# Seven 128-cubed zone products for each 256-cubed block product in two of three weight slices

## The chip, the cores and the metric

The kernel runs on one core of one Trainium2 chip. The metric is device time in microseconds, the median of several executions. One more execution is taken with the hardware profiler, and all views come from it.

## What is computed

One layer over 128 graphs of 128 nodes and 768 features, 12 heads of 64, all in fp32. The kernel's heads and weights are those of this reference, cut to what matters:

```python
h = jnp.maximum(_layernorm(x, axis=-1), 0.0)
q, k, v = (split_heads(h @ W + b) for W, b in ((Wq, bq), (Wk, bk), (Wv, bv)))   # W: 768 x 768
scores = einsum('bhqd,bhkd->bhqk', q, k) / 8 + beta * adj
scores = where(adj > 0, scores, -9e15)
out = einsum('bhqk,bhkd->bhqd', softmax(scores), v)
x = x + merge_heads(out)
```

## The kernel before

Four graphs make a group, and `direct` loops over 32 groups `G`. A group's activations are 512 rows of 768, cut into 2 x 3 blocks of 256 (`A00` to `A12`, held transposed). The weights are used in three slices of 768 columns: `qk0` (the first three 128-column blocks of Wq and of Wk side by side), `v`, and `qk1` (the other half of Wq and Wk). Each slice is cut into 3 x 3 blocks of 256 (`B00` to `B22`).

A slice takes 15 block products in place of 18 (`PRODUCTS`): sums of activation blocks (`SUMS_A`, made on VectorE by `sum_acts`, one set a group) are multiplied by sums of weight blocks (`SUMS_B`, made once, by `sum_weights` on VectorE or, for part of `qk0`, by accumulating DMAs on GpSimd's queue in `sum_by_dma`, and kept in SBUF). A product is added to one or two of the six results, with a sign. Products of one of four chains `a` to `d` add up in one PSUM bank, and after each product the partial sum of its chain goes out (`product`, L404 the matmuls): the first of a result by ScalarE with the bias (L426; for V by VectorE, L416), the others by VectorE adds into SBUF (L432, L421). Group 0 does its first slice as 18 plain products (`plain_slice`, L612) while the sums are being made.

The order within a slice is written by hand: after the product at position n, the functions listed in `todo[n]` are called. So the score matmuls of the slice before (`scores`, L454) come at position 1 of the next slice, followed by VectorE's cap and bias (L458) and ScalarE's exponentials (L461); the products of probabilities with V (`attend`, L494) are interleaved with matmuls of the slice by `turn()`, then come the division (L475, ScalarE's L478 in group 0), the residual add on GpSimd (L503) and the store (L504). The next group's rows are loaded (`load_x`, L162), normalised by ScalarE in place (`norm`, L334), transposed by VectorE (`to_hT`, L341) and summed (L347). From group 3 on the row statistics come from separate loads (`load_halves`, L301), and `row_moments` (called at the last position of `qk0`) spreads mean and scale over the partitions by 16 small DMAs (`block<-row`, L325).

A scheduler turns this into one queue for each engine: among the instructions that are ready it takes the one that comes first in the code, unless `tc.issue_after` puts it behind another; waits and buffer slots follow from the tiles. DMAs are issued from SyncE's queue (SP) but for a few; a DMA waits in that queue for the slot that it writes and for what it reads.

Of the kernel before, what the change touches and what calls it, by code (L numbers as in the profile page):

```python
# [17 lines left out]
P = 128  # L18
HEADS = 12
GRP = 4  # L20
# [11 lines left out]
def kernel(  # L32
# [64 lines left out]
BY_DMA = (  # L97
    ("T10", (None, "B12")), ("T2", ("B01", "B02", "B22")), ("T6", ("B00", "B02", "B22")), ("T0", (None, "B00")),
    ("T11", ("B11", "B12")),
)  # L100
DONE_BY_DMA = (1, 2, 3, 4, 6, 11)


# [7 lines left out]
AV_AT = (5, 8, 11)  # L111
WARM = 13

# [4 lines left out]
SUMS_AT = (5, 9, 6, 6, 7, 8, 9, 10, 11, 13, 14)  # L118


@with_exitstack
def direct(ctx, tc, x, adj, wq, bq, wk, bk, wv, bv, beta, out, bad):
# [27 lines left out]
    stat = ctx.enter_context(tc.tile_pool(name="stat", bufs=4))  # L150
    psum = ctx.enter_context(tc.tile_pool(name="psum", bufs=1, space=bass.MemoryType.PSUM))
# [4 lines left out]
    xg, A, biasT, vt, qk = {}, {}, {}, {}, {}  # L156

    def load_x(G, g, engines):
        t = xg[G, g] = work.tile([P, NB, QD], F32, tag="x", name=f"x_{G}_{g}")
        src = x[G * GRP + g].rearrange("(b i) (a f) -> a i b f", i=SQ, a=NB)  # L160
        for a in range(NB):
            engines[a % len(engines)].dma_start(t[a * SQ:(a + 1) * SQ], src[a])  # L162


    for g in range(2):
        t = xg[0, g] = work.tile([P, NB, QD], F32, tag="x", name=f"x_0_{g}")
# [16 lines left out]
    vring = [const.tile([P, 2 * GRP, VE], F32, name=f"v{i}") for i in range(7)]  # L183
# [5 lines left out]
    def load_block(sl, k, j, t, add=False):  # L189
        def part(w, at, n):  # L190
            return w.rearrange("(p c) n -> p c n", c=NC)[:, 2 * k:2 * k + 2, at:at + n]

        if sl == "v":
            nc.sync.dma_start(t, part(wv, j * 2 * P, 2 * P))
        else:
            oc = j + 3 * int(sl[2])
            for i, w in enumerate((wq, wk)):
                if add:
                    nc.gpsimd.dma_start(t[:, :, i * P:(i + 1) * P], part(w, oc * P, P), accum_op=ALU.add)
                else:  # L200
                    nc.sync.dma_start(t[:, :, i * P:(i + 1) * P], part(w, oc * P, P))

    def load_weights(sl, blocks=[f"B{k}{j}" for j in range(3) for k in range(3)]):
        for b in blocks:
            t = const.tile([P, 2, H2], F32, name=f"{sl}_{HOME.get(b, b)}")
            load_block(sl, int(b[1]), int(b[2]), t)
            wt[sl, b] = t

    def sum_by_dma(sl, step):

        for name, blocks in BY_DMA:
            if step < len(blocks):
                if (sl, name) not in wt:
                    raw = [r for r, home in HOME.items() if home == name]
                    wt[sl, name] = wt[sl, raw[0]] if raw else const.tile([P, 2, H2], F32, name=f"{sl}_{name}")
                b = blocks[step]
                if b:
                    load_block(sl, int(b[1]), int(b[2]), wt[sl, name], step > 0)

    def sum_weights(sl, n):  # L220
        name, a, b, sign = SUMS_B[n]
        if sl == "qk0" and n in DONE_BY_DMA:
            return
# [3 lines left out]
        if a[0] == "-":  # L227
            nc.vector.scalar_tensor_tensor(wt[sl, name], wt[sl, a[1:]], -1.0, wt[sl, b], op0=ALU.mult,
                                           op1=ALU.add if sign > 0 else ALU.subtract)
        else:  # L230
            nc.vector.tensor_tensor(wt[sl, name], wt[sl, a], wt[sl, b], ALU.add if sign > 0 else ALU.subtract)
# [11 lines left out]
    bqk = const.tile([P, 2, NC], F32, name="bqk")  # L243
# [92 lines left out]
    def to_hT(G, r, k):  # L336
        name = f"A{r}{k}"
        t = A[G, name] = work.tile([P, 2, H2], F32, tag=name, name=f"{name}_{G}", bufs=1 + (name in ("A01", "A02")))
        for g in range(2):
            src = xg[G, 2 * r + g].rearrange("p b (j c) -> p c b j", c=NC)[:, 2 * k:2 * k + 2]  # L340
            last = nc.vector.transpose(t[:, :, g * N:(g + 1) * N].rearrange("p c (b i) -> p c b i", i=SQ), src)  # L341
        return last

    def sum_acts(G, n):
# [3 lines left out]
        A[G, name] = t  # L348

# [37 lines left out]

    def product(G, sl, n, order):
# [8 lines left out]
        for i in range(2):  # L397
            for c in range(2):
                if sl == "v":
                    lhs, rhs = a[:, c, i * N:(i + 1) * N], b[:, c, :]  # L400
                else:
                    lhs, rhs = b[:, c, i * P:(i + 1) * P], a[:, c, :]
# [4 lines left out]
        for (r, j), sign in uses:  # L407
            key = (G, sl, r, j)
            if sl == "v":
                got = p.rearrange("p g (h d) -> p (g h) d", d=HD)  # L410
                if key not in vt:
                    vt[key] = vring[nv[0] % len(vring)]
                    nv[0] += 1
                    o4 = vt[key].rearrange("p (g h) e -> p g h e", g=2)[:, :, :, 0:HD]
                    bias = bv_b[:, j * 2 * P:(j + 1) * 2 * P].rearrange("p (h d) -> p h d", d=HD)
                    added[G] = nc.vector.tensor_tensor(o4, bias[:, None, :, :].to_broadcast([P, 2, 4, HD]),  # L416
                                                        p.rearrange("p g (h d) -> p g h d", d=HD),
                                                        ALU.add if sign > 0 else ALU.subtract)
                else:
                    o = vt[key][:, :, 0:HD]  # L420
                    added[G] = nc.vector.tensor_tensor(o, o, got, ALU.add if sign > 0 else ALU.subtract)  # L421
            elif key not in qk:
                t = qk[key] = work.tile([P, 2, H2], F32, tag="qk", name=f"{sl}_{G}_{r}_{j}", bufs=8)
# [19 lines left out]
    def scores(G, u):  # L443

        order = (3 * u, 3 * u + 2, 3 * u + 1)
        ps = {(oc, i): take() for oc in order for i in range(2)}
        for oc in order:
            for g in range(GRP):
                t = qk[G, f"qk{u}", g // 2, oc % 3]
                at = slice((g % 2) * N, (g % 2 + 1) * N)  # L450
                for i in range(2):
                    r = slice(i * HD, (i + 1) * HD)
                    for k in range(0, N, HD):
                        nc.tensor.matmul(ps[oc, i][k:k + HD, g * N:(g + 1) * N], t[r, 1, at][:, k:k + HD], t[r, 0, at],  # L454
# [10 lines left out]
    def weigh(G, oc, r, pa, o):  # L465
# [7 lines left out]
        def divide():  # L473
            if G:
                nc.vector.tensor_mul(o, pa[:, :, 0:HD], t[:, 1, :, None].to_broadcast([P, 4, HD]))  # L475
            else:
                for b in range(4):
                    nc.scalar.activation(o[:, b], pa[:, b, 0:HD], AF.Copy, scale=t[:, 1, b:b + 1])  # L478
# [106 lines left out]
    def attention(G, u):  # L585

        todo = {}
        for i, oc in enumerate((3 * u, 3 * u + 2, 3 * u + 1)):
            todo.setdefault(AV_AT[i] - 3, []).append(lambda oc=oc: load_xo(G, oc))
            todo.setdefault(AV_AT[i], []).append(lambda oc=oc: attend(G, oc))  # L590
        return todo

# [6 lines left out]
    def plain_slice(G, sl, todo):  # L599

        n = 0
        for r in range(2):
            for j in range(3):
# [3 lines left out]
                parts = (slice(0, N), slice(N, H2)) if r == j == 0 else (slice(0, H2),)  # L607
                for at, k in [(at, k) for at in parts for k in range(3)]:
                    a, b = A[G, f"A{r}{k}"], wt[sl, f"B{k}{j}"]
                    for i in range(2):  # L610
                        for c in range(2):
                            last = nc.tensor.matmul(p[:, i, at], b[:, c, i * P:(i + 1) * P], a[:, c, at],  # L612
                                                    start=(k == 0 and i == 0 and c == 0), stop=(c == 1),
                                                    skip_group_check=True)
# [5 lines left out]
                    if k == 2:  # L620
                        t = qk[G, sl, r, j] = work.tile([P, 2, H2], F32, tag="qk", name=f"{sl}_{G}_{r}_{j}", bufs=8)
                        oc = j + 3 * int(sl[2])
                        for i in range(2):
                            nc.scalar.activation(t[:, i, :], p[:, i, :], AF.Identity, bias=bqk[:, i, oc:oc + 1])
# [33 lines left out]
    def rows_2(g, mv, r):  # L658

        v = xg[0, g].rearrange("p b (j c) -> p c (b j)", c=NC)  # L660
        for k in range(3):
            n = work.tile([P, 2, P], F32, tag="e", name=f"rows_{g}_{k}", bufs=6)
            first["dve"] = nc.vector.tensor_scalar(n, v[:, 2 * k:2 * k + 2], mv[:, 0:1], r, op0=ALU.subtract,
# [22 lines left out]
    def second():  # L686
# [5 lines left out]
        nc.scalar.copy(bqk.rearrange("p i c -> p (i c)"), bank[:, 0:2 * NC])  # L692
        give(bank)

# [48 lines left out]
    for G in range(NG):  # L743
        todo = attention(G - 1, 1) if G else {}
# [9 lines left out]
        if G:  # L754
            todo.setdefault(SC_AT, []).insert(0, lambda: scores(G - 1, 1))
# [13 lines left out]
        if not G:  # L769
# [4 lines left out]
            for n in range(len(SUMS_A)):  # L774
                then(n + 5, lambda n=n: after(sum_acts, 0, n))
            for n in range(len(SUMS_B)):
                then(n // 2 + 5, lambda n=n: after(sum_weights, "v", n))
            plain_slice(0, "qk0", todo)
        else:
            if G == 1:  # L780
                for n in range(8, len(SUMS_B)):
                    then(n - 7, lambda n=n: behind_scores(sum_weights, "qk0", n))
                then(4, lambda: behind_scores(bias_2, 1, early[1]))
            slice_of(G, "qk0", todo)
        todo = {SC_AT: [lambda: scores(G, 0)]} if G else {}
        if G + 1 < NG:
# [13 lines left out]
            else:  # L800
                for n in range(len(SUMS_B)):
                    then(n, lambda n=n: behind_adds(sum_weights, "qk1", n))
                then(8, lambda: sum_by_dma("qk0", 0))
                then(10, lambda: early.append(behind_adds(bias_1, 0, adj_0)))
        slice_of(G, "v", todo)
# [180 lines left out]
```

## Time and profile before

| | |
|---|---|
| time, median of 3 runs | 2881.66 us (2881.62 to 2881.95) |
| profiled execution: span from first to last instruction | 2879.8 us |
| time of the profiled execution itself | not given beside its span; the median lies 1.9 us above the span |
| TensorE, weight loads, VectorE, ScalarE, GpSimd busy | 100%, 70%, 69%, 28%, 12% |
| DMA | 220.93 MB, 77 GB/s in the mean |

In the views below, a line of the groups or the timeline names the source line (L404 is line 404 of the kernel), the engine (PE TensorE, PEld its weight loads, DVE VectorE, ACT ScalarE, POOL GpSimd, SPq SyncE's DMA queue), the operation, and result <- inputs with shapes. In the groups there follow count, busy us, mean ns of one, and the engine's idle time just before with what ended most of it. In the timeline the first two numbers are the start and the length in us of a run of like instructions. In the busy times by stretch the columns are stretch, its length, then busy us and count of PE, PEld, DVE, ACT, POOL, then granted clock, DMA share and GB/s.

### The profile page before, as it was taken

The page shows a single profiled execution, that of the slowest core. Times are in us where ns is not written, and L with a number is a line of the kernel's source. Part 1 is how long each engine was busy: PE and PEld are TensorE (multiplying, and loading weights), DVE is VectorE, ACT ScalarE, POOL GpSimd, SP SyncE. Part 2 cuts the span into 40 slices and gives each one's busy share as a digit, 9 for nine tenths or more (in the row PEclk, how much of TensorE's full clock was granted, in tenths as well). Part 3 has the DMA queues.
Part 4 walks back from the last instruction along what each step waited for, and adds up shares of the span by engine and source line. Part 5 has one row for each costly group of instructions (what it writes and reads, how often), then busy time and mean ns, then how long its engine had stood idle before and what let it go on. Part 6 is the DMA issues. An engine that isn't in the chain of part 4 may idle for free.

```text
span 2879.8 us, 81472 instructions
## 1 busy us (share of the span) xinstructions
PE 2871.1 (100%) x35321; PEld 2010.1 (70%) x35321; DVE 1972.8 (69%) x4511; ACT 815.4 (28%) x1755; POOL 333.4 (12%) x319
## 2 busy tenths in 40 slices
PE   9999999999999999999999999999999999999999
PEld 7766667666676666767667766677666676666766
DVE  7867667676666666666766667667676676766665
ACT  1522222232332323313232232322222222323321
POOL 3111011110111110110101101011010111101100
PEclk9999999999999999999999999999999999999999
DMA  8222223222232222332223322233222232222311
GB/s 203 77 61 78 64 79 84 79 69 69 74 87 82 65 71 69 88 86 64 75 70 82 86 65 79 64 82 84 69 79 61 81 84 78 69 68 74 86 39 43
DMA packets 417363, 220.93 MB, mean 77 GB/s; under 512 B 109148, under 2 KB 416616, under 8 KB 417000
## 3 DMA queue, kind: packets, MB, share of 16 engines
q1 hardware_dynamic: 412864, 213.45, 27.4%
q8 instruction: 277, 4.54, 0.7%
q0 software_dynamic: 3808, 1.84, 0.5%
q14 instruction: 86, 0.70, 0.1%
q10 hardware_dynamic: 328, 0.40, 0.1%
HBM read 164.76 MB, written 50.33 MB: 75 GB/s over the span
## 4 chain that ended last, share of the span: by engine, by line


## 5 line engine op out<-in xcount | busy, mean ns | idle before, releaser
L404 PE MATMUL bank<-S,qk_T 128*64 128x256 f32 x7056 | 867.5, 380 | 0.0
L432 DVE TENSOR_TENSOR qk<-qk,bank 128x512 f32<-128x512 f32 (+1 forms) x631 | 425.2, 674 | 395.9 <-PE bank L404 394.0
L426 ACT ACTIVATE qk<-bank,bqk 128x256 f32<-128x256 f32 x756 | 316.5, 470 | 1132.7 <-PE bank L404 946.8
L494 PEld LDWEIGHTS bank<-v,e 128*64 128x64 f32 x6048 | 433.2, 137 | 220.4
L404 PEld LDWEIGHTS bank<-S,qk_T 128*64 128x64 f32 x7056 | 454.7, 137 | 173.3 <-ACT e L461 5.2
L404 PE MATMUL bank<-S,qk_B 128*64 128x256 f32 x4032 | 543.5, 380 | 0.3 <-ACT qk L426 0.3
L503 POOL TENSOR_TENSOR xo<-xo,o 128x512 f32<-128x512 f32 x189 | 252.6, 1336 | 2258.0 <-DVE o L475 1587.6
L404 PE MATMUL bank<-A,qk_T 128*64 128x256 f32 x4032 | 490.1, 379 | 0.0
L494 PE MATMUL bank<-v,e 128*64 128x65 f32 x6048 | 430.8, 221 | 0.0
L404 PE MATMUL bank<-v_T,S 128*64 128x256 f32 x3584 | 421.4, 380 | 0.0
L461 ACT ACTIVATE e<-e 128x512 f32<-128x512 f32 x378 | 227.8, 629 | 655.1 <-DVE e L458 654.5
L421 DVE TENSOR_TENSOR v<-v,bank 128x512 f32<-128x512 f32 x320 | 219.9, 687 | 233.0 <-PE bank L404 231.2
L404 PEld LDWEIGHTS bank<-v_T,S 128*64 128x64 f32 x3584 | 254.6, 137 | 130.4 <-issue 5.7
L404 PEld LDWEIGHTS bank<-A,qk_T 128*64 128x64 f32 x4032 | 262.8, 137 | 100.8 <-issue 0.2
L458 DVE SCALAR_TENSOR_TENSOR e<-bank,biasT 128x512 f32<-128x512 f32 x378 | 231.7, 681 | 85.2 <-PE bank L454 85.2
L404 PEld LDWEIGHTS bank<-S,qk_B 128*64 128x64 f32 x4032 | 236.2, 138 | 56.2 <-ACT qk L426 0.7
L404 PE MATMUL bank<-v_B,S 128*64 128x256 f32 x2048 | 243.2, 379 | 0.0
L404 PE MATMUL bank<-v_T,A 128*64 128x256 f32 x2048 | 238.1, 379 | 0.0
L334 ACT ACTIVATE x<-x,block 128x192 f32<-128x192 f32 x464 | 217.7, 536 | 63.3 <-DMA block<-row 60.3
L341 DVE STREAM_TRANSPOSE A<-x 128x256 f32<-128x256 f32 x378 | 213.1, 610 | 4.0 <-ACT x L334 3.9
L404 PEld LDWEIGHTS bank<-v_T,A 128*64 128x64 f32 x2048 | 147.3, 137 | 73.7
L404 PEld LDWEIGHTS bank<-v_B,S 128*64 128x64 f32 x2048 | 147.2, 137 | 73.6
(102 smaller groups left out, 1665.5 us busy)
## 6 DMA issues: line engine op xcount, KB each, us to landing
x<-in_x_dram SPq DMA_DIRECT2D x504, 96.0 KB, 2.6
xo<-in_x_dram SPq DMA_DIRECT2D x189, 256.0 KB, 3.0
out_dram<-xo SPq DMA_DIRECT2D x189, 256.0 KB, 2.4
half<-in_x_dram SPq DMA_DIRECT2D x232, 192.0 KB, 2.4
adj<-in_adj_dram SPq DMA_DIRECT2D x128, 64.0 KB, 2.4
block<-row SPq DMA_DIRECT2D x464, 1.0 KB, 1.7
qk_T<-in_L_gnn_Wq_dram SPq DMA_DIRECT2D x13, 128.0 KB, 4.1
qk_T<-in_L_gnn_Wk_dram SPq DMA_DIRECT2D x13, 128.0 KB, 4.5
```

The lines of the kernel that those rows point to most:

```text
L334: nc.scalar.activation(t, t, AF.Relu, bias=shift[G, n], scale=rstd[G, n])
L341: last = nc.vector.transpose(t[:, :, g * N:(g + 1) * N].rearrange("p c (b i) -> p c b i", i=SQ), src)
L404: nc.tensor.matmul(p[q:q + HD, i, :], lhs[:, q:q + HD], rhs, start=(first and i == 0 and c == 0), stop=(c == 1), skip_group_check=True)
L421: added[G] = nc.vector.tensor_tensor(o, o, got, ALU.add if sign > 0 else ALU.subtract)
L426: opened[0] = nc.scalar.activation(t[:, i, :], p[:, i, :], AF.Identity, bias=bqk[:, i, oc:oc + 1], scale=float(sign))
L432: added[G] = nc.vector.tensor_tensor(t[:, :, cols], t[:, :, cols], p[:, :, cols], ALU.add if sign > 0 else ALU.subtract)
L458: taken[0] = nc.vector.scalar_tensor_tensor(e, ps[oc, i].rearrange("p (g n) -> p g n", g=GRP), SCORE_CAP * ISCALE, biasT[G], op0=ALU.min, ...
L461: nc.scalar.activation(e, e, AF.Exp, scale=1.0 / ISCALE)
L494: nc.tensor.matmul(pa[q:q + HD, 2 * g + i, :], es[G, oc, i][:, 2 * r + g, q:q + HD], vt[G, "v", r, h // 4][:, 4 * g + h % 4, :], start=Tru ...
L503: nc.gpsimd.tensor_add(t, t, o.rearrange("p a (b j) d -> p (a b) (j d)", j=2))
```

## The change

In groups 1 to 31 the slices `qk0` and `v` are done by `slice_z` and `product_z`: a 256-cubed product is cut once more into 2 x 2 x 2 blocks of 128 and done as seven 128-cubed products ("zones") in place of eight. Four sums of 128 x 128 activation blocks are made per product on GpSimd (`inner`, called in the `qk1` slice before), the seven weight zones of a product (`T`, 128 x 7 x 128) are prepared in group 0 (`prepare`: VectorE's sums, ScalarE's copies, four GpSimd sums each), stored to a DRAM buffer (`kept`) and streamed back for each product (`load_T`) through five slots. A chain has two PSUM banks; the zones are summed apart over the whole slice, and `decode` on GpSimd combines the seven zones of a finished result into its four blocks. Group 0's `v` slice becomes plain. The features are assigned to partitions in another order, so each weight part is loaded by four DMAs of 32 rows and a pair of graphs is transposed in one instruction. The sums by DMA go, the division is done by ScalarE in all groups, and scores and attention come in another order and somewhat later. The diff, cut to its core:

```diff
-BY_DMA = (...)
+AV_Z = (7, 9, 12)
+ZORDER = (0, 4, 2, 8, 1, 6, 5, 3, 10, 7, 13, 9, 11, 12, 14)
+RING = 5
+INNER_AT = ((5, (1, 11, 12)), (6, (0,)), (7, (4, 2)), (8, (5,)), (9, (6,)), (10, (8, 3, 9)), (11, (7,)), (12, (10,)),
+            (14, (13, 14)))
...
+    def load_part(w, k, at, n, t):
+        src = w.rearrange("(a c j) n -> a j c n", a=NB, j=SQ)
+        for a in range(NB):
+            nc.sync.dma_start(t[a * SQ:(a + 1) * SQ], src[a][:, 2 * k:2 * k + 2, at:at + n])
...
+        def home(n):
+            return work.tile([P, 7, P], F32, tag="T", name=f"prep_{sl}_{n}", bufs=RING)
+        def rest(n, t):
+            e = nc.gpsimd
+            e.tensor_tensor(t[:, 2], t[:, 4], t[:, 1], ALU.subtract)
+            e.tensor_tensor(t[:, 6], t[:, 1], t[:, 0], ALU.subtract)
+            e.tensor_tensor(t[:, 1], t[:, 4], t[:, 6], ALU.subtract)
+            e.tensor_tensor(t[:, 5], t[:, 3], t[:, 1], ALU.subtract)
+            k = kept[sl, n] = dram.tile([P, 7, P], F32, name=f"kept_{sl}_{n}")
+            nc.sync.dma_start(k, t)
...
+    ring = [(G, sl, n) for G in range(1, NG) for sl in ("qk0", "v") for n in ZORDER]
+    def load_T():
+        if nt[0] < len(ring):
+            G, sl, n = ring[nt[0]]
+            nt[0] += 1
+            t = tz[G, sl, n] = work.tile([P, 7, P], F32, tag="T", name=f"T_{G}_{sl}_{n}", bufs=RING)
+            nc.sync.dma_start(t, kept[sl, n])
...
+    def inner(G, n):
+        a = A[G, PRODUCTS[n][0]]
+        t = SP[G, n] = work.tile([P, GRP, P], F32, tag=f"SP{ZORDER.index(n)}", name=f"SP{n}_{G}", bufs=1)
+        e = nc.gpsimd
+        e.tensor_tensor(t[:, 0], a[:, 0, N:H2], a[:, 1, N:H2], ALU.add)
+        e.tensor_tensor(t[:, 1], t[:, 0], a[:, 0, 0:N], ALU.subtract)
+        e.tensor_tensor(t[:, 2], a[:, 0, 0:N], a[:, 0, N:H2], ALU.subtract)
+        e.tensor_tensor(t[:, 3], a[:, 1, 0:N], t[:, 1], ALU.subtract)
...
+    def product_z(G, sl, n):
...
+        acts = (a[:, 0, 0:N], s[:, 1], s[:, 2], a[:, 1, 0:N], s[:, 3], a[:, 1, N:H2], s[:, 0])
+        for z in range(7):
+            lhs, rhs = (acts[z], b[:, z]) if sl == "v" else (b[:, z], acts[z])
+            for q in range(0, P, HD):
+                nc.tensor.matmul(p[z // 4][q:q + HD, z % 4, :], lhs[:, q:q + HD], rhs, start=(first and z % 4 == 0),
+                                 stop=True, skip_group_check=True)
+            turn()
+        load_T()
...
+                t = qk[key]
+                nc.vector.tensor_tensor(t[:, 0:4], t[:, 0:4], p[0], op)
+                added[G] = nc.vector.tensor_tensor(t[:, 4:7], t[:, 4:7], p[1][:, 0:3], op)
+            left[key] -= 1
+            if not left[key]:
+                decode(G, sl, r, j)
...
+    def decode(G, sl, r, j):
+        def twice(z):
+            return t[:, z:z + 1].to_broadcast([P, 2, P])
+        if sl != "v":
+            e.tensor_tensor(t[:, 1:4:2], t[:, 1:4:2], twice(0), ALU.add)
+            e.tensor_tensor(t[:, 2:5:2], t[:, 2:5:2], twice(1), ALU.add)
+            e.tensor_tensor(t[:, 4], t[:, 4], t[:, 6], ALU.add)
+            e.tensor_tensor(t[:, 5:7], t[:, 5:7], twice(2), ALU.add)
+            return
...
-            if G:
-                nc.vector.tensor_mul(o, pa[:, :, 0:HD], t[:, 1, :, None].to_broadcast([P, 4, HD]))
-            else:
-                for b in range(4):
-                    nc.scalar.activation(o[:, b], pa[:, b, 0:HD], AF.Copy, scale=t[:, 1, b:b + 1])
+            for b in range(4):
+                nc.scalar.activation(o[:, b], pa[:, b, 0:HD], AF.Copy, scale=t[:, 1, b:b + 1])
...
         if G:
-            todo.setdefault(SC_AT, []).insert(0, lambda: scores(G - 1, 1))
+            for n, order in ((1, (2, 0)), (2, (1,))):
+                todo.setdefault(n, []).insert(0, lambda order=order: scores(G - 1, 1, order))
...
-            slice_of(G, "qk0", todo)
+            slice_z(G, "qk0", todo)
...
+            for at, ns in INNER_AT:
+                for n in ns:
+                    then(at, lambda n=n: inner(G + 1, n))
```

More of the change, by code (lines that the diff above doesn't have):

```diff
@@ L408, in product @@
             key = (G, sl, r, j)
[L409 to L423, printed above, removed]
+            if key not in qk:
+                t = qk[key] = home_qk(*key)
                 oc = j + 3 * int(sl[2])
@@ L773, in direct, with step @@
             then(4, lambda: half(2))
[L774 to L777, printed above, removed]
+            prep = deque(prepare("qk0") + prepare("v"))
+            def step(behind, count):
+                for _ in range(count):
+                    if prep:
+                        behind(prep.popleft())
+            for n in range(5, 18):
+                then(n, lambda n=n: step(after, 1 + n % 2))
             plain_slice(0, "qk0", todo)
```

254 lines of the change are left out of this document (178 added, 76 removed).

## The prediction

> **What bounds the kernel now.** First the page: the span and the busy shares, then the groups.
>
> ```profile
> PE 2871.1 (100%) x35321; PEld 2010.1 (70%) x35321; DVE 1972.8 (69%) x4511; ACT 815.4 (28%) x1755; POOL 333.4 (12%) x319
> ...
> L503 POOL TENSOR_TENSOR xo<-xo,o 128x512 f32<-128x512 f32 x189 | 252.6, 1336 | 2258.0 <-DVE o L475 1587.6
> ...
> L475 DVE TENSOR_TENSOR o<-bank,sm 128x256 f32<-128x256 f32 x369 | 153.6, 416 | 0.0
> ```
>
> TensorE never rests, at a granted clock of 1.00; GpSimd is nearly free. The list of waits names no wait of TensorE over 3 us. The score matmuls (L454) recur after 31.63 and 57.53 us, so a group takes 89.16 us. Busy time in one such period (its first two columns are the stretch and TensorE):
>
> ```profile
> 184.00:215.63 31.63, 31.63 (x436) 22.48 (x434) 21.21 (x53) 8.54 (x18) 4.73 (x4) 1.00 0.36 98
> 215.63:273.20 57.57, 57.57 (x676) 39.79 (x674) 39.94 (x88) 16.66 (x35) 5.03 (x5) 1.00 0.25 64
> ```
>
> Then the timeline, for the matmuls, SyncE's queue, and one place where VectorE meets GpSimd.
>
> ```profile
> 1003.03 1.90 PE L404 MATMUL bank<-S,qk_B 128*64 128x256 f32 x16
> 1004.76 1.90 PE L404 MATMUL bank<-S,qk_T 128*64 128x256 f32 x16
> ...
> 1006.92 0.28 PE L494 MATMUL bank<-v,e 128*64 128x65 f32 x4
> 1007.03 0.60 PE L404 MATMUL bank<-S,qk_B 128*64 128x256 f32 x4
> 1007.47 0.28 PE L494 MATMUL bank<-v,e 128*64 128x65 f32 x4
> ```
>
> A product (16 matmuls) starts every 1.73 us, 0.108 a matmul. Four of 65 columns and four of 256 take 0.55, so the four short ones 0.12, though each loads new weights: no floor from weight loads down to 0.03 us.
>
> ```profile
> 7.46 3.80 SPq L162 DMA_DIRECT2D x<-in_x_dram  x8
> ...
> 1117.04 1.07 SPq L355 DMA_DIRECT2D adj<-in_adj_dram  x2
> 1118.51 10.85 SPq L325 DMA_DIRECT2D block<-row  x16
> 1129.41 0.58 SPq L441 DMA_DIRECT2D xo<-in_x_dram  x1
> ```
>
> SyncE needs 0.475 us to issue one DMA of 32 rows, and sits 10.85 us over the 16 small ones of `row_moments` (464 in all, so in 29 groups). Today nothing on the path waits behind them.
>
> ```profile
> 185.45 0.68 DVE L347 TENSOR_TENSOR S<-S,A 128x512 f32<-128x512 f32 x1
> 186.05 0.68 DVE L432 TENSOR_TENSOR qk<-qk,bank 128x512 f32<-128x512 f32 x1
> 186.65 1.17 DVE L347 TENSOR_TENSOR S<-A,A 128x512 f32<-128x512 f32 x1
> ...
> 185.61 1.66 POOL L503 TENSOR_TENSOR xo<-xo,o 128x512 f32<-128x512 f32 x1 [5.81 <-DVE o L475]
> ```
>
> A GpSimd add (1.277 at the median) and a VectorE sum with both inputs in SBUF (0.685) hold each other up: 1.66 and 1.17. The add that reads PSUM (L432) is untouched.
>
> **The change, part by part.**
>
> *Matmuls.* A zone product has 28 matmuls of 128 columns. Between 65 columns (0.029) and 256 (0.108) a straight line gives 0.0545: 1.53 us a product. 30 products a group: 30 x (1.73 - 1.53) = **-5.9 us a group**. Bounds: 0.054 by pure proportion, and 0.057 if weight loads set the pace (2010.1 us busy over 35,321 of them), 1.60 a product and -3.9.
>
> *The weight stream.* 30 loads `kept` to `T`, 448 KB each, five slots. A load is issued when the product that read the slot is done, so it has four products (6.1 us) to land. A `half` load (192 KB) lands in 2.4 us; 256 KB more at the 221 GB/s that the first 31 us show at a DMA share of 0.82 (270 in full) make 3.4. Hidden by those 6.1 us, unless SyncE is busy. (A load that waits for its slot holds up what is queued behind it on SyncE, `xo` loads and stores, by a product at most; these have slack.) It is: the 16 `block<-row` DMAs are emitted at the end of the first Q/K slice, ahead of all the V loads, so they go first as soon as the row values exist, some 1 to 3 us into V. From there five filled slots last five products (7.65) and 0.9 to 2.6 of score matmuls; the next load lands 10.85 + 3.4 = 14.25 later. TensorE stands 4.0 to 5.7, I take **+4.7 a group** in 29 groups. At nothing if loads slip in between; a row where something slips in does not exist, so 0 is the lower end.
>
> *GpSimd.* Adds of 128x512 take 1.277, of 128x256 0.728 (L564), of 128x4 0.201 (L321): 0.184 plus 0.0021 a column, 0.456 for 128. `inner`: 60 x 0.456 = 27.4; `decode` for Q/K 6 x (3 x 0.728 + 0.456) = 15.8, for V 6 x (0.728 + 5 x 0.456) = 18.0; `xo` 7.7: 69 us a group, up from 9.8. The eleven `sum_acts` in the same slice as `inner` now meet it: up to 0.6 each, 76 of about 90. It keeps up on average. At the end of the first Q/K slice the leftover of `inner`, then six decodes (15.8) and three `xo` adds run about 8 us into V, where the last scores want them after 6.3: +1.5, bounds 0 and 5.
>
> *VectorE, ScalarE.* Two adds (0.675 and, between 256 at 0.418 and 512 at 0.675, 0.55 for 384) replace one: +0.55 on 10 of 16 uses in Q/K; in V 10 x 1.22 + 12 x 0.29 against 16 x 0.687, +4.7. Away: twelve L475 (-5.0) and half of the transposes' fixed time (-3). VectorE goes from 61 to 64 plus some 4 of waiting for GpSimd. ScalarE gains the divisions (48 x 0.233, from L478's 11.2 busy in 48) and V's openings: 25 to 47. Both fit; but zone products of one chain lie two apart, so an evacuation has 1.5 us where it had 1.7 or more for half the work. With the DMA queue fuller, +0.8, bounds 0 and 3.
>
> *With one answer:* the accumulating DMAs on GpSimd's queue (L199, 24.8 us in group 0) and VectorE's sums for them go, off the path; scores in two parts, later attention and the other x layout move work without adding to TensorE's.
>
> *Steady state:* 89.16 - 5.9 + 4.7 + 1.5 + 0.8 = 90.2, +1.1 in each of 29 groups: +31. Groups 1 and 31 have no such run: -3.6 each.
>
> *The start.* Raw weights come in 180 DMAs in place of 45. Eight issues a block, 3.8 us: the ninth Q/K block is issued at 2.3 + 80 x 0.475 = 40.3 and lands at 43, so the first slice ends near 59 in place of 42: +17. V as 18 plain products: +5.2. The V and second-slice blocks keep SyncE until 40.3 + 3.3 + 108 x 0.475 = 95. The `kept` stores are emitted later and wait behind them; with five slots only five tiles are prepared till then, and VectorE and ScalarE stand in order behind the sixth. The other 25 need 4 x 0.456 us of GpSimd each, 46: done near 145, first zone product near 155; before, group 1 began at 101 (its scores, two products in, at 104.9). **+55**, bounds +22 (the stores are not held back) and +85.
>
> *Sum:* 2879.8 + 55 + 31 - 7 = 2958. The median (2881.7) lies 1.9 above this execution's span: **2960**.
>
> *A rule against it.* The 26 matmuls of the warm-up (L679) take 5.48 us, 0.21 each; 24 of the same shape at 9.05 (L612) take 2.84, 0.12. TensorE is slow after rest, though the page shows a clock of 1.00 there: such a spell costs 5.48 x (1 - 0.12/0.21) = 2.4. No later gap is over 0.5 us, so no row shows whether one of 4.7 is rest enough; that is the third rival. [...]
>
> **The rivals.**
>
> 1. *The stream is hidden* (faster): the loads go before or between the small DMAs. For: the issue order is the scheduler's, and loads are seen to go out well ahead of where the code has them (x in the slice before). Against: 16 in one piece, and the V loads can't be ready earlier than their slots. Every group then gains 5.9 - 2.3: 2879.8 - 31 x 3.6 + 55 + 1.9 = 2825.
> 2. *GpSimd becomes the bound* (slower): if its short adds take 0.6 in place of 0.456 (strided halves, dependent neighbours), it needs 76 + 90 x 0.14 + 7 = 95 a group. Decides from 90. No short add of this kind is in the trace; 2960 + 29 x 4.8 = 3100.
> 3. *TensorE is slow again after each stall*, as at the start: 2960 + 29 x 2.4 = 3030. For: the stall is longer than any gap today. Against: the warm-up came after a far longer rest.
> 4. *Bandwidth*: 30 x 448 KB in the 53 us of two zone slices are 260 GB/s, beside 64 to 98 now. Packets of 3 KB take 119 ns at the least in the trace's records, 154 at the median; at the second, a load takes 1.44 of all engines and the slices some 4 us more: 3075.
>
> **How the numbers follow.** Chances: forecast 0.45, hidden 0.27, GpSimd 0.10, clock 0.08, bandwidth 0.08, and 0.02 that the terms cancel. The forecast's own range, from the bounds of the stalls and the start, is 2870 to 3045. The whole range, 2790 (rival 1 with the start at +22) to 3095, leaves a tenth on each side. Under 0.2% (6 us) this kernel's runs can't tell from no change: faster 0.28 (rival 1 and a little of the forecast), same 0.04, slower 0.68.
>
> **What would show it.** Right: TensorE idle 4 to 6 us in each V slice, ended by a DMA of T; 16 `block<-row` in one piece just before; zone products 1.53 us apart elsewhere; first zone product after 140. Wrong: T loads between the small DMAs, score matmuls less than 86 us apart, GpSimd busy over 95%, or 28 matmuls taking more than 1.6.

## The result, and the profile after

The changed kernel takes 3600.97 us (median of three, 3597.29 to 3607.5) against 2881.66: a ratio of 1.250, 95% interval 1.248 to 1.252. The prediction was 2960, 2790 to 3095. The sign was right; the time lies 500 us above the range. The profiled execution has a span of 3599.0 us.

First its page: the shares, the two groups of zone matmuls that read a streamed tile first, and the loads of T.

```profile
PE 2921.5 (81%) x46385; PEld 2519.5 (70%) x46385; DVE 2114.0 (59%) x4755; ACT 1361.9 (38%) x3999; POOL 2334.8 (65%) x4146
...
L494 PE MATMUL bank<-S,T_qk 128*64 128x128 f32 x4092 | 445.4, 295 | 244.3 <-DMA T_qk<-kept_qk 243.5
L494 PE MATMUL bank<-T_v,S 128*64 128x128 f32 x4092 | 432.8, 293 | 221.0 <-DMA T_v<-kept_v 219.4
...
T_qk<-kept_qk SPq DMA_DIRECT2D x465, 448.0 KB, 5.0
```

TensorE was busy the whole span before; now it is at 81%, its weight loads at 70%, and no other engine is above 65%. A kernel in which nothing is full is held up by waits. TensorE's list of waits names them: its first three rows, with the total, the number and the longest.

```profile
PE bank L494 <- DMA T_qk<-kept_qk: 244.8, 32, 10.0
PE bank L494 <- DMA T_v<-kept_v: 219.4, 34, 8.3
PE bank L494 <- POOL SP L428: 46.9, 29, 2.2
```

About one long stand in the first Q/K slice and one in V, in each group. Busy time by stretches of one group: the zone products of the first Q/K slice, the first part of V, the middle of V with its stand, the rest with the second Q/K slice, and the whole.

```profile
1401.04:1437.90 36.86, 28.07 (x558) 27.10 (x558) 20.42 (x50) 15.15 (x50) 24.86 (x44) 0.86 0.78 249
1437.90:1454.00 16.10, 13.19 (x260) 11.38 (x258) 9.52 (x28) 8.10 (x20) 8.60 (x13) 1.00 0.54 154
1454.00:1475.50 21.50, 13.84 (x184) 12.96 (x186) 6.13 (x13) 9.95 (x23) 3.89 (x8) 0.76 0.58 186
1475.50:1511.60 36.10, 34.37 (x467) 26.25 (x463) 29.29 (x60) 8.72 (x31) 34.75 (x64) 1.00 0.41 130
1401.04:1511.60 110.56, 89.47 (x1455) 77.68 (x1453) 65.36 (x147) 41.93 (x123) 72.10 (x128) 0.91 0.59 184
```

The group takes 110.6 us where it took 89.2. TensorE stands still for 21.1 of them (110.56 less 89.47); a stand is such a stretch. The granted clock (the last column but two) is 0.86 and 0.76 where the two long stands are. The timeline of TensorE shows both stands:

```profile
1408.55 0.39 PE L494 MATMUL bank<-SP,T_qk 128*64 128x128 f32 x4
1417.67 0.70 PE L494 MATMUL bank<-S,T_qk 128*64 128x128 f32 x4 [8.74 <-DMA T_qk<-kept_qk]
...
1463.51 0.69 PE L494 MATMUL bank<-T_v,S 128*64 128x128 f32 x4 [7.66 <-DMA T_v<-kept_v]
```

Four zone matmuls take 0.39 us ahead of a stand and 0.70 behind it. Windows over the second part of each stand and what follows it, and shorter ones behind the stands, give the granted clock:

```profile
1411.40:1421.60 10.20, 3.93 (x38) 3.96 (x40) 0.00 (x0) 1.38 (x4) 2.94 (x6) 0.50 0.90 294
1417.60:1421.70 4.10, 4.03 (x39) 4.06 (x41) 0.00 (x0) 1.39 (x4) 0.00 (x0) 0.51 0.99 355
1422.00:1424.30 2.30, 2.30 (x46) 2.30 (x44) 0.53 (x1) 1.29 (x4) 0.00 (x0) 1.00 1.01 337
1463.50:1467.50 4.00, 3.99 (x38) 3.99 (x40) 0.57 (x2) 0.86 (x3) 0.00 (x0) 0.50 0.91 337
1459.20:1469.40 10.20, 5.89 (x56) 5.89 (x58) 0.86 (x3) 5.07 (x13) 0.00 (x0) 0.50 0.78 262
```

The clock is halved (0.50) in the second part of a stand, and stays so behind it: TensorE works 3.9 us at half clock behind the first stand and 5.9 us behind the one in V, so 2.0 and 2.9 us are lost there; after the first it is seen at 1.00 again. Why the loads were late is read in SyncE's queue, of the same group:

```profile
1399.20 0.41 SPq L651 DMA_DIRECT2D out_dram<-xo  x1
...
1407.03 0.40 SPq L651 DMA_DIRECT2D out_dram<-xo  x1
1407.47 2.40 SPq L169 DMA_DIRECT2D x<-in_x_dram  x2
...
1412.22 0.40 SPq L651 DMA_DIRECT2D out_dram<-xo  x1
1412.71 0.98 SPq L305 DMA_DIRECT2D T_qk<-kept_qk  x2
...
1446.08 0.39 SPq L651 DMA_DIRECT2D out_dram<-xo  x1
1446.52 1.62 SPq L436 DMA_DIRECT2D adj<-in_adj_dram  x3
1448.24 10.99 SPq L399 DMA_DIRECT2D block<-row  x16
1459.34 15.26 SPq L305 DMA_DIRECT2D T_v<-kept_v  x10
...
1487.26 4.48 SPq L169 DMA_DIRECT2D x<-in_x_dram  x8
1510.57 0.41 SPq L651 DMA_DIRECT2D out_dram<-xo  x1
```

and in what it waited for:

```profile
SPq L651 <- POOL SP L426: 614.7, 59, 28.2
SPq L651 <- POOL xo L650: 355.6, 96, 19.9
```

The middle part is the run of small DMAs that the prediction spoke of: 10.99 us in one piece, ahead of ten T loads. The first and the last part of this view it did not foresee. From 1491.7 to 1510.6 SyncE issues nothing, for it holds the store of a finished output block, and that store waits for the residual add on GpSimd (L650). The list names an add of `inner` (L426) for most of the stores' waits: the residual add stands in GpSimd's order among the 60 short adds of `inner`. The next view has, of GpSimd and ScalarE, the row values that the 16 small DMAs spread, then the last divisions that the add behind the pause needs, and that add:

```profile
1446.70 0.20 POOL L395 TENSOR_TENSOR row<-meanrow,row 128x4 f32<-128x4 f32 x1
...
1494.84 0.93 ACT L625 ACTIVATE o<-bank,sm 128x64 f32<-128x64 f32 x4 [0.19 <-DVE sm L619]
...
1509.28 1.26 POOL L650 TENSOR_TENSOR xo<-xo,o 128x512 f32<-128x512 f32 x1
```

The divisions are done at 1495.77, and GpSimd starts 24 more adds of `inner` before the residual add. The row values too are late: GpSimd makes them among the decodes, so the small DMAs could not have gone before 1446.9. A group has six stores. Three of them come around the start of the first Q/K slice, the x loads stand between them, and the slice's next T loads, behind the five that are in their slots, go out after the third, at 1412.71, some 5 us before the stand ends.

### The profile page after: what moved, and what is told of

Read it like the earlier page. It is cut to its first block, busy times and chain, and to the rows that moved or that the text cites. A ratio compares the mean times of both kernels' runs of the same rounds, so it can differ in the third digit from the quotient of the medians.

```text
span 3599.0 us, 114220 instructions
## 1 busy us (share of the span) xinstructions
PE 2921.5 (81%) x46385; PEld 2519.5 (70%) x46385; DVE 2114.0 (59%) x4755; ACT 1361.9 (38%) x3999; POOL 2334.8 (65%) x4146
## 4 chain that ended last, share of the span: by engine, by line
## 5 line engine op out<-in xcount | busy, mean ns | idle before, releaser
L494 PE MATMUL bank<-SP,T_qk 128*64 128x128 f32 x7440 | 709.5, 288 | 46.9 <-POOL SP L428 46.9
L494 PE MATMUL bank<-T_v,SP 128*64 128x128 f32 x7440 | 679.3, 285 | 0.0
L625 ACT ACTIVATE o<-bank,sm 128x64 f32<-128x64 f32 x1524 | 348.4, 318 | 849.2 <-DVE sm L619 448.9
L494 PE MATMUL bank<-S,T_qk 128*64 128x128 f32 x4092 | 445.4, 295 | 244.3 <-DMA T_qk<-kept_qk 243.5
L494 PE MATMUL bank<-T_v,S 128*64 128x128 f32 x4092 | 432.8, 293 | 221.0 <-DMA T_v<-kept_v 219.4
L519 DVE TENSOR_TENSOR qk<-qk,bank 128x512 f32<-128x512 f32 x310 | 208.5, 672 | 559.0 <-PE bank L494 391.0
L494 PEld LDWEIGHTS bank<-SP,T_qk 128*64 128x64 f32 x7440 | 482.9, 147 | 53.0 <-POOL SP L428 53.0
L494 PEld LDWEIGHTS bank<-T_v,SP 128*64 128x64 f32 x7440 | 486.4, 145 | 0.0
L494 PEld LDWEIGHTS bank<-S,T_qk 128*64 128x64 f32 x4092 | 281.4, 150 | 261.5 <-issue 254.5
L494 PEld LDWEIGHTS bank<-T_v,S 128*64 128x64 f32 x4092 | 275.1, 148 | 247.0 <-DMA T_v<-kept_v 228.0
L568 PE MATMUL bank<-S,qk_T 128*64 128x256 f32 x3584 | 442.2, 380 | 2.6 <-DVE qk L583 1.7
L583 DVE TENSOR_TENSOR qk<-qk,bank 128x512 f32<-128x512 f32 x321 | 219.1, 683 | 137.6 <-PE bank L568 116.5
L568 PE MATMUL bank<-A,qk_T 128*64 128x256 f32 x2048 | 253.4, 384 | 48.3 <-ACT v L509 41.2
L568 PE MATMUL bank<-S,qk_B 128*64 128x256 f32 x2048 | 278.8, 384 | 13.5 <-DVE qk L583 12.7
L568 PEld LDWEIGHTS bank<-S,qk_T 128*64 128x64 f32 x3584 | 231.1, 137 | 82.5 <-DVE qk L583 1.8
```

Source lines behind the costliest of these rows:

```text
L494: nc.tensor.matmul(p[z // 4][q:q + HD, z % 4, :], lhs[:, q:q + HD], rhs, start=(first and z % 4 == 0), stop=True, skip_group_check=True)
L519: nc.vector.tensor_tensor(t[:, 0:4], t[:, 0:4], p[0], op)
L568: nc.tensor.matmul(p[q:q + HD, i, :], lhs[:, q:q + HD], rhs, start=(first and i == 0 and c == 0), stop=(c == 1), skip_group_check=True)
L583: added[G] = nc.vector.tensor_tensor(t[:, :, cols], t[:, :, cols], p[:, :, cols], ALU.add if sign > 0 else ALU.subtract)
```

## The experiments

Theory 1: the T loads are late because of what stands ahead of them in SyncE's order. Theory 2: they are late because 448 KB take 5.0 us to land and four products cover 6.1. The period below is the distance between the first zone products of the groups 4 and 28, over 24; the stand is TensorE's idle time in it, in stretches over 0.1 us. Some kernels leave work out: e4_nostream loads five tiles T in all and uses them with every product; f2, f3 and f4 leave out 15 of the 16 small DMAs of a group.

| kernel | time, us | ratio to before | period, us | stand, us |
|---|---|---|---|---|
| changed | 3600.97 | 1.250 [1.248, 1.252] | 110.06 | 20.08 |
| e1_store | 3719.02 | 1.290 [1.288, 1.292] | 114.14 | 22.69 |
| e2_block | 3557.54 | 1.234 [1.232, 1.236] | 108.52 | 18.89 |
| e3_both | 3731.72 | 1.295 [1.292, 1.297] | 114.05 | 23.30 |
| e4_nostream | 3233.76 | 1.121 [1.119, 1.123] | 97.99 | 9.25 |
| f1_xo_dve | 3194.06 | 1.109 [1.107, 1.111] | 96.14 | 8.65 |
| f2_onerow | 3303.86 | 1.146 [1.144, 1.148] | 99.58 | 10.61 |
| f3_xo_dve_onerow | 2972.61 | 1.032 [1.031, 1.034] | 88.58 | 2.86 |
| f4_and_divide | 3003.42 | 1.042 [1.040, 1.044] | 89.73 | 3.92 |
| h1_spread | 2958.47 | 1.026 [1.024, 1.028] | 88.21 | 2.60 |
| h2_spread_kept | 2912.79 | 1.011 [1.010, 1.013] | 88.08 | 2.41 |
| h3_bounce | 2865.49 | 0.994 [0.992, 0.995] | 86.60 | 1.54 |
| h4_bounce_wk | 2862.59 | 0.994 [0.992, 0.995] | 86.26 | 1.26 |

### The store on GpSimd's queue (e1_store)

```diff
-        nc.sync.dma_start(out[G * GRP:(G + 1) * GRP, :, ...], t)
+        nc.gpsimd.dma_start(out[G * GRP:(G + 1) * GRP, :, ...], t)
```

> One part of the traffic is moved: the store of a finished output block is issued from GpSimd's queue, right behind the add that makes it, in place of SyncE's. In the changed kernel a group takes 110.6 us: 83.3 of matmuls at their pace, 21.1 in which TensorE stands, 6.2 in which its matmuls run at about half pace behind the two long stands. Theory 1 (SyncE's order: the store waits on SyncE for GpSimd, up to 28 us, and the T loads stand behind it): the stand of 8.2 us in the first Q/K slice shrinks under 2, with half of the slow pace; about 100 to 102 us a group, 3600 - 29 x 9.5 = 3325 us (3270 to 3390). Theory 2 (the T loads land late because 448 KB take 5 us and four products cover 6.1): nothing moves but GpSimd's issue time; 3570 to 3640.

Slower: a miss for both theories. SyncE's waits in this kernel say why:

```profile
SPq L592 <- DMA out_dram<-xo: 1076.4, 117, 31.2
```

The load of the next `xo` block (three buffers) now waits on SyncE for the store to free its buffer, 31.2 us at the longest, and the T loads stand behind that load. The wait was not taken away; it moved one instruction on. The small DMAs, with no store ahead of them, now waited for the row values from GpSimd (L399 on L395, 205.5 us in 29 waits). That the add itself is late became the next theory.

### The small DMAs on ScalarE's queue (e2_block)

```diff
-                nc.sync.dma_start(to[a * SQ:(a + 1) * SQ, b], t[b * SQ:(b + 1) * SQ])
+                nc.scalar.dma_start(to[a * SQ:(a + 1) * SQ, b], t[b * SQ:(b + 1) * SQ])
```

> Only the 16 small block<-row DMAs of a group are moved, from SyncE's queue to ScalarE's. Theory 1 (SyncE's order): the stand of 7.9 us in V was put down to their 10.85 us in one piece; it falls to 2 at most (a store that waits 6 us for GpSimd is ahead of them and stays), ScalarE issues for 11 us more (42 to 53 of 110): 102 to 104 us a group, 3600 - 29 x 7.5 = 3380 us (3320 to 3460). Theory 2 (landing time): 3570 to 3640. Rival: ScalarE's openings now stand behind the 16 issues and TensorE waits for a bank there instead: 3550 to 3650.

The rival in the expectation is what happened. TensorE's wait for T in V fell from 219.4 us to 5.9, and in its place came one for ScalarE's openings, 314.4 in 30 waits. (An opening, L507 or L509, is the first copy of a result's zones from PSUM to SBUF.) ScalarE's timeline in one group:

```profile
1434.70 10.21 ACTq L399 DMA_DIRECT2D block<-row  x16
1445.01 0.49 ACT L507 ACTIVATE v<-bank 128x384 f32<-128x384 f32 x1 [15.50 <-DMA block<-row]
```

The opening of a zone product is queued behind 16 issues of 10.2 us in all, and these behind the row values: of the 15.5 us, 5.2 pass before the first issue, at 1434.70, just after GpSimd has made the values (L395, 1434.46 to 1434.67).

### Both moves together (e3_both)

> The two moves together. Theory 1 (SyncE's order): both long stands of TensorE go, and with them the slow pace behind each; 88 to 93 us a group, 3600 - 29 x 20 = 3020 us (2960 to 3120). Theory 2 (landing time): over 3500. A third reading, that GpSimd (72 us busy in a group) takes over as the wait once the stands are gone, would leave 95 to 100 us a group: 3150 to 3300.

3731.72 us: both moved waits are there at once (270.3 us for T in the first Q/K slice, 311.1 for ScalarE's openings). None of the three readings had that; in both moves the wait still stood ahead of something that TensorE needed.

### No stream (e4_nostream)

```diff
-            t = tz[G, sl, n] = work.tile([P, 7, P], F32, tag="T", ..., bufs=RING)
-            nc.sync.dma_start(t, kept[sl, n])
+            if nt[0] <= RING:
+                t = work.tile([P, 7, P], F32, tag="T", ..., bufs=RING)
+                nc.sync.dma_start(t, kept[sl, n])
+                held.append(t)
+            tz[G, sl, n] = held[(nt[0] - 1) % RING]
```

The general code path behind the kernel, which wrong products could call, is shut off too.

> No stream: five prepared weight tiles are loaded once and every zone product reads one of them, so 925 loads of 448 KB are left out (the products are formed with the wrong weights, and the fallback is not entered). All else is as in the changed kernel. Theory 1 and 2 both: no stand on T is left, and without them no slow pace; what remains are the short waits for GpSimd (4.5 us a group): 88 to 90 us a group, and the start 105 us later than before: 2881.7 + 105 - 29 x 0.3 = 2980 us (2940 to 3040). If a group still takes over 95 us, something else than the stream bounds it (GpSimd first of all), and the T loads were only the last of several waits: 3150 or more.

With five loads of T in all a group still takes 98.0 us: over 95, so the loads were only the last of several waits. TensorE's timeline in V, and the row of ScalarE's waits that explains it:

```profile
1529.48 0.69 PE L498 MATMUL bank<-T_qk,S 128*64 128x128 f32 x4 [5.23 <-DVE v L523]
```

```profile
ACT x L412 <- DMA block<-row: 164.8, 66, 6.5
```

ScalarE normalises the next group's x in V, and that waits for the same small DMAs. The openings of V are queued behind it, VectorE's zone adds wait for the openings, and TensorE for the adds (L523, 149.5 us in 31 waits). In the kernel before, V's first evacuations were VectorE's (L416); ScalarE's normalisation waited for the small DMAs there too (60.3 us), and TensorE was 100% busy.

### The residual add on VectorE (f1_xo_dve)

```diff
-        nc.gpsimd.tensor_add(t, t, o.rearrange("p a (b j) d -> p (a b) (j d)", j=2))
+        nc.vector.tensor_add(t, t, o.rearrange("p a (b j) d -> p (a b) (j d)", j=2))
```

> The residual add of a finished output block goes from GpSimd to VectorE, nothing else. With the store on GpSimd's queue the wait only changed its place: the next xo load on SyncE waited up to 31 us for that store and the T loads stood behind it again. So theory 1 now says: it is the add itself that is late, since it stands in GpSimd's order behind the 60 short adds of the next group's inner sums. On VectorE it comes right after the division: the 8.2 us stand in the first Q/K slice and the slow pace behind it (2 to 3 us) go, 99 to 101 us a group, 3600 - 29 x 10 = 3310 us (3250 to 3400). Theory 2 (T loads of 448 KB simply land too late): the stand stays, 3560 to 3650. VectorE takes 4 us a group more.

407 us less, more than theory 1 said. The wait for T in the first Q/K slice is gone from TensorE's list; that in V is still there (186.2 us). SyncE's stores still wait 414 us in all for the add, in place of 1053, but no longer so late that a T load of that slice is held up. The other 3 us a group fit waits that went with it: the one for `inner` (46.9 us before) and ScalarE's for its output buffer; no run separates them.

### One small DMA in place of 16 (f2_onerow), and both (f3_xo_dve_onerow)

```diff
-        for b in range(NB):
-            for a in range(NB):
-                nc.sync.dma_start(to[a * SQ:(a + 1) * SQ, b], t[b * SQ:(b + 1) * SQ])
+        nc.sync.dma_start(to, t)
```

> One small DMA a group in place of the 16 block<-row (15 are left out, so most rows are normalised with another row's values). Theory 1: SyncE is free 10 us earlier in V, the 7.9 us stand and its slow pace (2 to 3) go, and the V openings on ScalarE no longer stand behind normalisations that wait for these DMAs: 98 to 101 us a group, 3600 - 29 x 10.5 = 3295 us (3230 to 3400). Theory 2: the stand stays at 5 or more, over 3500. The store that waits for GpSimd ahead of them may keep some 3 us of it.

> Both of these together. Theory 1: no long stand of TensorE is left and its clock stays full; 88 to 92 us a group, start 105 us late: 2881.7 + 105 + 29 x 1 = 3015 us (2960 to 3100), below the kernel without any stream (3234), where the small DMAs were still in the way of the openings. If GpSimd's and VectorE's orders hold the products up as well, 95 us a group, 3160.

As theory 1 said for both. With 297 and 407 us for each alone, the two together take off 628. Over ten groups of the last, TensorE stands for 26 of 880 us, at a clock of 1.00, while T streams on at 233 GB/s:

```profile
400.00:1280.00 880.00, 853.91 (x14634) 743.79 (x14632) 683.87 (x1529) 424.83 (x1249) 683.15 (x1230) 1.00 0.74 233
```

This kernel, with the stream, is 9.4 us a group shorter than the one without it. A load of T lands no faster in it than in the changed kernel (5.0 us for the Q/K slice, 5.7 for V), and TensorE stands 2.9 us a group. The stream costs at most that when its loads go out in time: theory 2 falls.

### The division back on VectorE (f4_and_divide)

```diff
         def divide():
+            if G:
+                nc.vector.tensor_mul(o, pa[:, :, 0:HD], t[:, 1, :, None].to_broadcast([P, 4, HD]))
+            else:
```

> As the last one, and the divisions go back from ScalarE to VectorE, as in the kernel before. ScalarE waited 450 to 650 us in all for VectorE's reciprocals, with the openings of the zone products queued behind. If that chain still costs TensorE something, 1 to 4 us a group come off the last kernel (30 to 110 us less); if it only filled ScalarE's free time, VectorE's 5 us more a group show as 0 to 3 us a group more (0 to 90 us more).

30.8 us slower, 1.15 a group, as the second reading had it: with the waits on SyncE out of the way, division on ScalarE is a gain on its own.

### The small DMAs spread out (h1_spread), and the kept stores moved (h2_spread_kept)

```diff
-                nc.sync.dma_start(to[a * SQ:(a + 1) * SQ, b], t[b * SQ:(b + 1) * SQ])
+                small.append(lambda a=a, b=b: nc.sync.dma_start(to[a * SQ:(a + 1) * SQ, b], t[b * SQ:(b + 1) * SQ]))
...
-                then(14, lambda: row_moments(G + 1))
+                then(12, lambda: row_moments(G + 1))
...
+            for n in range(8 if G > 1 else 0):
+                then(n, send_small)      # two of them behind each product of V
...
-            nc.sync.dma_start(k, t)      # kept, in both places (h2_spread_kept only)
+            nc.gpsimd.dma_start(k, t)
```

> All the work is done again. The residual add is on VectorE, and the 16 small DMAs stay on SyncE but go out two behind each of the first eight products of V, with the row statistics one or two products earlier, so that they are never in one piece ahead of a T load. Theory 1 (order in SyncE's queue, not the number of transfers): close to the kernel with one small DMA a group (2973 us); two small issues and a T issue are 1.7 us where a product lasts 1.53, so the queue falls behind by 0.2 us a product: 88 to 91 us a group, 2970 to 3060, I take 3000 us. If the number of small DMAs matters and not their place, the stand in V is back: 3150 to 3200 as with the add alone (3194).

> As the last one, and the 30 stores of prepared weight tiles go out on GpSimd's queue, behind the sums that make them, in place of SyncE's, where they stand behind all 180 weight loads until 101 us. The first zone product came at 206 us, 105 later than group 1 began before, and GpSimd was idle from 27 to 103 us and busy from there to 200. If the stores' place in SyncE's queue is what holds the preparation back, GpSimd starts near 45 us, and 35 to 55 us come off: 2930 to 2965 us, about 2950. If GpSimd's own issue (1.07 us for each store) and the order of its work set the end of the preparation, less than 15 us come off.

Sixteen small DMAs two at a time (2958 us, below the range expected) cost no more than a single one (2973): not their number was the cost, but when and where they stood in the queue. As their row values are also made two products earlier here, the time and the place are not told apart. The kept stores are worth 45.7 us, 39 of them at the start: the first zone product comes at 166.4 us in place of 205.3. The first 200 us in two windows, of the changed kernel and then of h2_spread_kept, tell it in GpSimd's column (the fifth):

```profile
0.00:100.00 100.00, 88.54 (x515) 74.05 (x517) 35.35 (x71) 16.44 (x40) 17.49 (x44) 0.93 0.36 93
100.00:200.00 100.00, 38.85 (x351) 26.93 (x346) 53.94 (x104) 21.25 (x69) 86.51 (x162) 0.66 0.44 159
```

```profile
0.00:100.00 100.00, 75.47 (x359) 64.46 (x359) 39.83 (x73) 18.10 (x54) 60.80 (x130) 0.93 0.56 176
100.00:200.00 100.00, 75.98 (x1120) 63.56 (x1124) 82.90 (x178) 38.15 (x115) 73.90 (x129) 0.83 0.71 214
```

### Rows through DRAM (h3_bounce), and half of the late weights from ScalarE (h4_bounce_wk)

```diff
+        d = dram.tile([P, 2, GRP], F32, name=f"rows_{G}")
+        nc.gpsimd.dma_start(d, t)
+        for a in range(NB):
+            small.append(lambda a=a: nc.sync.dma_start(to[a * SQ:(a + 1) * SQ], d.rearrange("(b s) r g -> s b r g", s=SQ)))
...
+                for n in range(9):       # h4_bounce_wk only: Wk of the second slice, on nc.scalar
+                    then(n // 3, lambda n=n: load_wk1(AS_SUMMED[n]))
```

> As the kernel with the spread small DMAs and the prepared tiles stored from GpSimd's queue (2913 us), but the row values go through DRAM: one store of 128 rows on GpSimd's queue and four loads on SyncE, in place of 16 DMAs on SyncE. There TensorE still waited 37 us in all for T in V (60 times, 1.3 at most), as SyncE had two small DMAs and a load to issue in each product. If these waits are SyncE's issue time, 20 to 37 us come off: 2880 us (2870 to 2900). If they are the loads' landing time, it stays at 2905 to 2920.

> As the last one, and half of the 72 loads of the second Q/K slice's weights are issued by ScalarE during the first V slice, in place of SyncE. At the start TensorE waited 19 us, from 87 to 106, for sums of these weights, whose last load SyncE issued at 108. If SyncE's issue time (0.46 us a DMA) sets that, SyncE is done 17 us earlier and 12 to 22 us come off the last kernel: about 2863 us (2850 to 2885), below the kernel before (2881.7). If ScalarE's 17 us of issue push back the preparation instead, it gains under 5 us.

h3_bounce leaves no work out and is 0.6% shorter than the kernel before: 0.994 [0.992, 0.995]. It gained 47 us where 20 to 37 were expected; TensorE's waits for T_v over the groups fell from 37.3 us to 3.2, and the issue order in V is now

```profile
1414.44 3.13 SPq L305 DMA_DIRECT2D T_v<-kept_v  x3
1417.66 2.44 SPq L402 DMA_DIRECT2D block<-rows  x3
1420.20 0.38 SPq L305 DMA_DIRECT2D T_v<-kept_v  x1
```

Where the other 13 us come from was not told apart.

h4_bounce_wk lies on the 2863 us expected, but by luck: h3_bounce came out 15 us shorter than the 2880 it was reckoned from, and the move itself gained 2.9 us, within the spread of the two (2861.0 to 2872.4, 2861.3 to 2866.0), where 12 to 22 were expected. The second reading (under 5 us) is what happened. TensorE's waits for sums of these weights fell from 22.9 us to 5.1, but ScalarE issued its 36 loads from 6.9 to 28.3 us, mostly ahead of its own first evacuations; the long run of the first slice's matmuls began at 38.99 us in place of 32.42, TensorE then waited 15.1 us for V's results (L611 on L787), and the first zone product came at 166.7 us in place of 166.9.

## Why the prediction was wrong

**The sum.** Start and groups account for it: the first zone product came at 206.2 us where 155 was forecast (+51), and 30 periods of 110.06 where 90.2 was forecast give +596; together 647, against 641 in the span (3599 less 2958). Of the 19.9 us that a period takes more than forecast, the mean over the groups 4 to 28 gives 8.2 to the stand in the first Q/K slice, 4.5 to the half clock, 2.8 to the stand in V, 1.8 to the matmuls and 1.6 to waits for `inner`; the rest is in small pieces.

**The step that failed** is the sentence in brackets of the weight stream: "A load that waits for its slot holds up what is queued behind it on SyncE, `xo` loads and stores, by a product at most; these have slack". It asked what stands behind a T load, and not what a T load stands behind. The wait of a store for the residual add was already in the trace of before, in the list of what SyncE waited for:

```profile
SPq L504 <- POOL xo L503: 490.6, 186, 33.2
```

There 490.6 us of it, 33.2 at the longest, cost TensorE nothing (it was 100% busy), for no load with a deadline stood behind it. In the changed kernel the stores wait 1053 us (614.7 and 355.6 in the rows shown, 82.3 in one more), and the T loads of the first Q/K slice stand behind them. The prediction's GpSimd part places three of a group's six `xo` adds, behind the decodes and some 8 us late, and follows them to the scores only (+1.5), not to the store that waits on SyncE; the three that stand among `inner`, a slice earlier, it does not place. So it put the first Q/K slice's stand at nothing; it is 8.7 us in the group shown and 8.2 in the mean, and f1_xo_dve, which moves the add alone, took 13.9 a group away.

**The other terms of a group.**

*The stand in V* was right in place and in the run of 16 that makes it, and mis-sized: 7.66 us here and 7.5 in the mean for 4.7. A V load takes 4.7 us to land for 3.4 estimated. And the row values existed only 9.0 us into V (1446.9 against 1437.9), where 1 to 3 were assumed, since GpSimd makes them among the decodes; a store that waited for GpSimd until 1446.08 and three adjacency loads stood ahead as well, and the 16 went 10.3 us into V.

*Clock:* rival 3 came true, within the forecast's own mechanism, where it had been given 0.08 as a case of its own. Of a period, 89.98 us are busy in the changed kernel and 85.06 in h3_bounce, whose clock is 1.00 over ten groups: 4.9 us more, of which 4.5 are half of the 9.0 us that TensorE works at half clock in a period. That is 2.2 us a stand, close to rival 3's 2.4, but behind two stands in each group. The granted clock behind the two stands shown is 0.50, over 3.9 and 5.9 us of work; no sharp length of a stand at which that begins was seen (below).

*Matmuls:* a zone product takes 1.53 us undisturbed (28 matmuls from 1396.06 to 1397.59). Yet h3_bounce's 85.06 busy us are 4.1 below 89.16, not 5.9: inside the bounds given, near the lower; why was not told apart.

*GpSimd* needed 72.1 us a group for 76 forecast, and its 128-column add takes 0.46 as worked out; rival 2 did not happen as worded (GpSimd full), but GpSimd's order did the harm at 65%. The last scores' wait for decodes (L604 on L540), forecast at 1.5, was 0.8; zone products waited 1.6 for the sums of `inner` (L494 on L428), which no term has.

*Bandwidth* (rival 4): the DMA engines were at 0.59 in a group, and at 0.74 in f3_xo_dve_onerow at full pace; they fill only in the catch-up behind a stand (0.99).

*VectorE and ScalarE,* +0.8: TensorE's list has 41.2 us in 29 waits for an opening of V (L568 on L509), 1.4 a group; that opening stood behind a normalisation that waited for the small DMAs, the chain that e4_nostream shows at 5.2 us.

**The start.** +55 was forecast, and the first zone product came 105 us later than group 1 began before. The kept stores were held until 101 us as forecast (95). The step that failed is "done near 145": it counted 46 us of GpSimd for the weights and left out the 27 us of `inner` for group 1, in the same order; the last tiles were stored at 196.9. The rest of these 96 us is mostly 12 us in which GpSimd stood idle and some 10 for adds that took up to 0.98 us where VectorE's sums ran beside them.

**Of the signs it named,** the run of 16, the stand in V ended by a DMA of T (7.7 us, outside the 4 to 6 named), products 1.53 us apart and a first zone product after 140 were all seen. They bore out its mechanism and could not show its size: none of them looked at the first Q/K slice.

## What to carry to other kernels

A load with a deadline shares its queue's order with everything else there (ten loads of T stood behind 10.99 us of small DMAs): for each DMA ahead of it ask which engine it waits for, and where in that engine's own order the awaited instruction now stands. Slow work added to an idle engine (GpSimd, from 12% to 65% busy) made its old, small jobs late, and whoever waits for them (the stores, from 490.6 us in all to 1053). When a wait is found, make the awaited work earlier; moving the waiting instruction to another queue moved the wait (e1_store, e2_block), and moving the add (f1_xo_dve) made it early enough. A wait that costs nothing today is worth a look in the trace: the stores' wait cost TensorE nothing until loads with a deadline were queued behind it.

## What the runs showed of the hardware

The granted clock of the changed kernel is 0.50 or 1.00 in the record. Around its 59 long stands (5.7 us and more, from 240 us on) the halved stretches last 6.83 us (25 of them), 10.24 (33) or 13.65 (1). They outlast the stand by 2.7 to 6.0 us, 4.3 in the mean, and zone matmuls run 0.107 us apart there in place of 0.055: a long stand costs about 2.2 us more than itself, half of the 4.3.

In the same trace, from 240 us to the last 60, with the length of a stand measured from one matmul's start to the next: each of the 57 long stands that began at full clock, 6.4 us and more so measured, had halved clock when the matmuls resumed. No stand lies between 2.8 and 6.3 us. Of 14 between 2.0 and 2.8 us, four had it 0.3 to 1.3 us after that; two of these took 2.43 and 2.45 us, and one of 2.61 did not have it. So no sharp length at which it begins is seen. Twelve of the 14 lie within about 5 us of another stand, and what one of them does alone is not shown.
